# State-space scans with one state per 128 channels in place of four states by 32 channels, and a feed-forward convolution divided between TensorE quarters and VectorE

## The chip, the cores and the metric

The program runs on one core of a Trainium2 chip. The metric is the device time of one execution in microseconds (us), taken as the median over several runs. A core has a matrix engine (TensorE; PE in the profile, its weight loads PEld), a vector engine (VectorE, DVE), an activation engine (ScalarE, ACT), a general engine (GpSimd, POOL) and a queue that issues the transfers (SyncE, SP). They run side by side and wait for each other through semaphores. SBUF is the on-chip memory of 128 partitions; PSUM is the memory into which TensorE writes.

## What is computed

Four layers follow each other on an image tensor x of shape (4, 64, 128, 128), all in float32. Layers 0 and 3 hold a selective state-space model ("Mamba"): a causal short convolution, then for each of 128 inner channels a recurrence over the tokens, with 16 states per channel in layer 0 and 64 in layer 3. There are 65,536 tokens, one sequence in layer 0 and four of 16,384 in layer 3.

```python
xc = silu(conv(xh)); delta = softplus(dt @ dt_proj_w.T + dt_proj_b); A = -exp(A_log)
def step(h, t):                       # h: (128 channels, N states)
    d, b, c, u = t
    h = h * exp(d[:, None] * A) + (d * u)[:, None] * b[None, :]
    return h, h @ c
y = (ys + xc * D) * silu(z)
```

After its Mamba part layer 3 ends with a feed-forward block: 64 channels go to 256 by a matrix product, a 3x3 depthwise convolution with bias and GELU follows, and a second product goes back to 64 channels. Layer 1 (a transform with small matrix products and a gradient measure) and layer 2 (3x3 convolutions with a gate) are the same in both kernels.

## The kernel before

The tokens of a Mamba layer are cut into chunks of TC = 1024, that is 64 chunks per layer. VectorE has one instruction that runs the recurrence `h = da*h + bx` along the free dimension for 128 partitions at once (`tensor_tensor_scan`, line 346). The kernel puts four states by 32 channels on the 128 partitions. A **group** g is four states, and j counts the four blocks of 32 channels, so a chunk has 16/4*4 = 16 scans in layer 0 and 64/4*4 = 64 in layer 3. One scan and what belongs to it is called a **unit** here: 64*16 + 64*64 = 5120 units in all. A unit of before is, in `_Mamba.run`:

```python
nc.scalar.activation(da, c["dl"][j], AF.Exp, scale=self.A[:, j, g : g + 1])   # L339, ScalarE
nc.vector.tensor_mul(bx, c["du"][j], b)                                       # L341, VectorE, bx and b in PSUM
nc.vector.tensor_tensor_scan(hs, da, bx, st, ALU.mult, ALU.add)               # L346, VectorE
nc.gpsimd.tensor_copy(st, hs[:, TC - 1 : TC])                                 # L347, GpSimd
nc.gpsimd.tensor_mul(hs, hs, cb)                                              # L348, GpSimd
```

`b` and `cb` are the rows B and C of the group's four states, spread over 32 partitions each by TensorE (`_B`, line 278, into PSUM; `_C`, lines 209 and 290, copied to SBUF by ScalarE). They serve all four j of a group, and `b` has a single buffer. `_sums` (line 310) then adds the four states by a matrix product with a selection matrix, into 32 partitions of y for each j. `dl` and `du` need every channel four times, so delta and delta*xc go to a DRAM scratch and come back broadcast (512 KB transfers on the SP queue).

`prepare` makes xc, silu(z) and delta of a chunk; `behind` closes a chunk (gate, projection, normalisation, store). Both are generators: `run` advances them between the units of the chunk in hand, so that the end of chunk i-1 and the start of chunk i+1 are written between the units of chunk i. The softplus's four terms are added by TensorE (line 209 with e, u, l, pos). The order on each engine comes from a tile framework, which schedules by the order of the program's text, by dependencies and free buffers, and sets the semaphores.

`layer3_ffn` works on 32 strips of 16 image rows. For each of two halves t of 128 channels it expands (`ph`, line 1124; bias by VectorE, line 1125), applies the depthwise convolution as nine products with 128x128 diagonal matrices for each four rows (`pd`, line 1138), GELU on ScalarE (line 1145), and the way back (`po`, line 1153; bias and residual on VectorE, line 1157).

Of the kernel before, what the change touches and what calls it, by code (L numbers as in the profile page):

```python
# [17 lines left out]
P = 128  # L18
# [6 lines left out]
NQ, DD = 4, 32  # L25
ND = DI // DD
SET6 = "natural_log_exp_and_others"
# [9 lines left out]
def _const_table():  # L37
# [46 lines left out]
        "sel": np.tile(np.eye(DD), (NQ, 1)),  # L84
        "neye": -eye,
# [44 lines left out]
class _Mamba:  # L130
# [4 lines left out]

    def __init__(self, ctx, tc, K, nst, w):
        nc = self.nc = tc.nc
        self.tc = tc
        self.K, self.nst, self.ng = K, nst, nst // NQ
        cp = self.cp = ctx.enter_context(tc.tile_pool(name="mc", bufs=1))
        self.wp = ctx.enter_context(tc.tile_pool(name="mw", bufs=2))
        self.dram = ctx.enter_context(tc.tile_pool(name="md", bufs=2, space=DRAM))
        self.bp = ctx.enter_context(tc.tile_pool(name="mb", bufs=1, space=PSUM))  # L150
# [4 lines left out]
        for k in range(2):  # L155
# [12 lines left out]
        wbc = cp.tile([P, 2 * nst], F32, name="wbc")  # L168
        nc.sync.dma_start(wbc, w["xp_bcT"])
        self.spread = cp.tile([P, 2 * self.ng, NQ, DD], F32, name="spread")  # L170
        nc.vector.tensor_copy(
            self.spread.rearrange("p g q e -> p (g q) e"), wbc.unsqueeze(2).to_broadcast([P, 2 * nst, DD])
        )
# [5 lines left out]
        pm = self.pm()  # L179
# [8 lines left out]
        self.conv_b, self.dt_b = cols["conv_b"], cols["dt_b"]  # L188
        self.dD = cp.tile([P, P], F32, name="dD")
        nc.vector.tensor_scalar(self.dD, K.eye, cols["D"], None, ALU.mult)  # L190
        self.A = cp.tile([P, ND, self.ng], F32, name="A")
        with nc.allow_non_contiguous_dma(reason="the states on the partitions"):
            for q in range(NQ):
                for j in range(ND):
                    nc.sync.dma_start(
                        self.A[DD * q : DD * (q + 1), j, :],
                        w["A_log"][DD * j : DD * (j + 1), :].rearrange("e (g q) -> e g q", q=NQ)[:, :, q],
                    )
        nc.scalar.activation(self.A, self.A, AF.Exp)
        nc.vector.tensor_scalar_mul(self.A, self.A, -1.0)  # L200
        self.state = cp.tile([P, ND, self.ng], F32, name="state")

    def pm(self):
        return self.misc.tile([P, 512], F32, name="pm", tag="pm")

    def mm(self, pairs):
        pm = self.pm()
        for i, (l, r) in enumerate(pairs):
            self.nc.tensor.matmul(pm, l, r, start=i == 0, stop=i == len(pairs) - 1)  # L209
        return pm  # L210

    def t(self, name, bufs=None, w=TC):
        return self.wp.tile([P, w], F32, name=name, tag=name, bufs=bufs)


    def prepare(self, c, S, before_silu=None):

        nc, K = self.nc, self.K
        cols = [slice(512 * h, 512 * (h + 1)) for h in range(NH)]
        xc, sz = c["xc"], c["sz"] = self.t("xc"), self.t("sz")  # L220
        for h in range(NH):
            a = 512 * h
            pm = self.mm([(self.taps[0], S[:, a : a + 512]), (self.taps[1], S[:, a + 2 : a + 514])])
            nc.scalar.activation(xc[:, cols[h]], pm, AF.Identity, bias=self.conv_b)
            yield
        for h in range(NH):
            pm = self.mm([(self.wz, S[:, 512 * h + 2 : 512 * h + 514])])
            at = nc.scalar.copy(sz[:, cols[h]], pm)
            if h < NH - 1:
                yield  # L230

        tc = self.tc
        with tc.high_priority():
            if before_silu:
                at = before_silu(at)
            for t in (xc, sz):
                with tc.issue_after(at.ins):
                    at = nc.scalar.activation(t, t, AF.Silu)
            with tc.issue_after(at.ins):
                nc.scalar.preload_act_table_set(SET6)  # L240
        yield


        pos, e, l, u = (self.t(k, 1) for k in ("pos", "e", "l", "u"))
        for h in range(NH):
            pm = self.mm([(self.wdt, xc[:, cols[h]])])
            nc.scalar.activation(e[:, cols[h]], pm, AF.Abs, bias=self.dt_b)
            nc.scalar.activation(pos[:, cols[h]], pm, AF.Relu, bias=self.dt_b)
            yield
        nc.scalar.activation(e, e, AF.Exp, scale=-1.0)  # L250
        nc.scalar.activation(l, e, AF.Ln, bias=1.0)

        nc.gpsimd.tensor_scalar(u, e, 1.0, 1.0, ALU.add, ALU.subtract)
        yield
        for h in range(NH):
            k = cols[h]
            pm = self.mm([(K.eye, e[:, k]), (K.neye, u[:, k]), (K.eye, l[:, k]), (K.eye, pos[:, k])])
            nc.scalar.copy(l[:, k], pm)  # L258
            yield
        d2 = self.dram.tile([2, DI, TC], F32, name="d2", tag="d2")  # L260
        nc.sync.dma_start(d2[0], l)
        nc.gpsimd.tensor_mul(u, l, xc)
        nc.sync.dma_start(d2[1], u)
        yield
        c["dl"], c["du"] = [], []
        for j in range(ND):
            for i, (k, bufs) in enumerate((("dl", 6), ("du", 6))):
                t = self.t(k, bufs)
                nc.sync.dma_start(
                    t, d2[i, DD * j : DD * (j + 1), :].unsqueeze(0).to_broadcast([NQ, DD, TC])  # L270
                )
                c[k].append(t)
        yield


    def _spread(self, k, xc, out):
        for h in range(NH):
            self.nc.tensor.matmul(  # L278
                out(h),
                self.spread[:, k].rearrange("p q e -> p (q e)"),  # L280
                xc[:, 512 * h : 512 * (h + 1)],
                start=True,
                stop=True,
            )

    def _C(self, c, g):
        cb = self.t("cb", 2)
        for h in range(NH):
            pm = self.mm([(self.spread[:, self.ng + g].rearrange("p q e -> p (q e)"), c["xc"][:, 512 * h : 512 * (h + 1)])])
            self.nc.scalar.copy(cb[:, 512 * h : 512 * (h + 1)], pm)  # L290
        return cb

    def _B(self, c, g):
        b = self.bp.tile([P, TC], F32, name="bb", tag="bb")
        self._spread(g, c["xc"], lambda h: b[:, 512 * h : 512 * (h + 1)])
        return b

    def _sums(self, c, g, hcs):

        nc, K = self.nc, self.K  # L300
        cols = [slice(512 * h, 512 * (h + 1)) for h in range(NH)]
        if g == 0:
            c["y"] = self.bp.tile([P, TC], F32, name="y", tag="y")
        for k in cols:
            if g == 0:
                for j in range(ND):
                    e = slice(DD * j, DD * (j + 1))
                    nc.tensor.matmul(c["y"][e, k], self.dD[:, e], c["xc"][:, k], start=True, stop=False)
            for j, hc in enumerate(hcs):
                nc.tensor.matmul(  # L310
                    c["y"][DD * j : DD * (j + 1), k], K.sel, hc[:, k], start=False, stop=g == self.ng - 1
                )

    def run(self, chunks, ahead, behind):

        nc = self.nc
        for c in chunks[:1]:
            for _ in ahead(c):
                pass
        owed = None  # L320
        for i, c in enumerate(chunks):
            if c.get("reset"):
                nc.gpsimd.memset(self.state, 0.0)  # L323

            def pieces():
                if i:
                    yield from behind(chunks[i - 1])
                if i + 1 < len(chunks):
                    yield from ahead(chunks[i + 1])

            side = pieces()
            b, cb = self._B(c, 0), self._C(c, 0)
            n = 0
            for g in range(self.ng):
                hcs = []
                nxt = None
                for j in range(ND):
                    da = self.t("da", 3)
                    nc.scalar.activation(da, c["dl"][j], AF.Exp, scale=self.A[:, j, g : g + 1])  # L339
                    bx = self.bp.tile([P, TC], F32, name="bx", tag="bx")  # L340
                    nc.vector.tensor_mul(bx, c["du"][j], b)  # L341
                    if j == ND - 1 and g + 1 < self.ng:
                        b = self._B(c, g + 1)
                    hs = self.t("hs", 7)
                    st = self.state[:, j, g : g + 1]
                    nc.vector.tensor_tensor_scan(hs, da, bx, st, ALU.mult, ALU.add)  # L346
                    nc.gpsimd.tensor_copy(st, hs[:, TC - 1 : TC])  # L347
                    nc.gpsimd.tensor_mul(hs, hs, cb)  # L348
                    hcs.append(hs)
                    if j == 0 and owed:  # L350
# [910 lines left out]
```

## Time and profile before

| what | value |
|---|---|
| median of 3 runs | 30958.74 us (30957.97 to 30961.4) |
| profiled execution: its time, its span | 30961.4 us, 30959.5 us |
| busy, share of the span | PE 72%, DVE 63%, POOL 47%, ACT 32% |
| granted TensorE clock, mean | 0.823 |
| layer 0 | 0 to 5755 us |
| layers 1 and 2, first convolutions of layer 3 | 5755 to 9456 us |
| Mamba of layer 3 | 9456 to 28550 us |
| feed-forward block | 28550 to 30959.5 us |

The borders of the stages are read from the timeline, at the last or first instruction of the stage. A row of the profile that names an instruction group gives the line, the engine, the operation, output and inputs by the program's names, the shapes as partitions x elements, how often it occurred, busy time and mean duration, and the engine's idle time just before with what ended it. A float32 matrix product of the program shows as two matmul records, so counts of matmuls are twice those of the code. Durations of matmuls overlap, since they are pipelined; the distance between two starts says what one costs.

### The profile page before, as it was taken

The numbers are of one execution on the slowest core, as the hardware profiler recorded it, in microseconds if no ns is written. First come the engines' busy times: TensorE is split into PE (matmuls) and PEld (weight loads), VectorE is DVE, ScalarE is ACT, GpSimd is POOL, SyncE is SP. The second block draws the span as 40 slices with busy tenths as digits, with TensorE's granted clock in tenths as the row PEclk, the third lists the DMA queues.
The fourth block names the chain that finished last, engine by engine and source line by source line (L and its number), as shares of the span: only waits on it lengthen the run. The fifth ranks groups of instructions, "written<-read, shape, count | busy, mean of one in ns | idle before, by whom it ended". The sixth has DMA issues, their size and how long they took to land.

```text
span 30959.5 us, 165906 instructions
## 1 busy us (share of the span) xinstructions
PE 22294.9 (72%) x54602; PEld 7060.7 (23%) x54602; DVE 19538.9 (63%) x11726; ACT 10006.5 (32%) x11580; POOL 14702.2 (47%) x11431
## 2 busy tenths in 40 slices
PE   6666666378997666666666666666666666666999
PEld 1111111165442111111111111111111111111444
DVE  6666666721005777777777777777777777776111
ACT  4444444201012333333333333333333333332000
POOL 5555555600003556555555555655655556554000
PEclk8888888679998778777787777877877778777999
DMA  2111111100100000000000000000000000000000
GB/s 74 70 72 72 70 71 72 48 33 26 44 23 33 23 22 27 22 23 23 24 25 23 22 24 23 24 23 22 27 22 23 23 22 27 23 21 17 22 22 20
DMA packets 369246, 1024.19 MB, mean 33 GB/s; under 512 B 53552, under 2 KB 105984, under 8 KB 363136
## 3 DMA queue, kind: packets, MB, share of 16 engines
q1 hardware_dynamic: 368384, 1013.58, 9.6%
q8 instruction: 433, 7.09, 0.1%
q14 instruction: 429, 3.51, 0.0%
HBM read 761.78 MB, written 251.66 MB: 33 GB/s over the span
## 4 chain that ended last, share of the span: by engine, by line
PE 34%; POOL 25%; issue 12%; DVE 8%; ACT 1%; DMA 0%; SPq 0%; POOLq 0%; DVEq 0%; ACTq 0%
POOL hs L348 22%; PE y L310 7%; PE cv L859 6%; PE pd L1138 6%; PE bb L278 6%; PE pm L209 4%; DVE hs L346 3%; DVE bx L341 2%; POOL state L347 2%; PE ph L1124 1%; PE p L814 1%; PE p L803 0%; PE po L1153 0%; PE pm L379 0%; PE p L772 0%
## 5 line engine op out<-in xcount | busy, mean ns | idle before, releaser
L310 PE MATMUL y<-hs,cst 128*32 128x512 f32 x20480 | 8009.9, 708 | 6203.5 <-POOL hs L348 6199.0
L346 DVE TENSOR_TENSOR_SCAN hs<-da,state,bx 128x1024 f32<-128x1024 f32 x5120 | 12012.9, 2346 | 696.5 <-DVE bx L341 15.1
L348 POOL TENSOR_TENSOR hs<-hs,cb 128x1024 f32<-128x1024 f32 x5120 | 12029.1, 2349 | 416.0 <-POOL state L347 5.7
L341 DVE TENSOR_TENSOR bx<-du,bb 128x1024 f32<-128x1024 f32 x5120 | 6289.2, 1228 | 5628.3 <-PE bb L278 4198.6
L339 ACT ACTIVATE da<-dl,A 128x1024 f32<-128x1024 f32 x5120 | 5875.2, 1149 | 12101.0 <-DVE hs L346 10337.2
L347 POOL COPY state<-hs 128x1 f32<-128x1 f32 x5120 | 939.1, 183 | 8551.9 <-DVE hs L346 5856.6
L310 PEld LDWEIGHTS y<-hs,cst 128*32 128x32 f32 x20480 | 1108.9, 117 | 12159.7 <-POOL hs L348 10055.4
L278 PE MATMUL bb<-xc,spread 128*128 128x512 f32 x5120 | 3513.5, 821 | 109.0 <-DVE bx L341 109.0
L209 PE MATMUL pm<-xc,spread 128*128 128x512 f32 x5120 | 2598.6, 621 | 85.2 <-ACT l L258 85.2
L859 PE MATMUL cv<-img,cw 128*128 128x512 f32 x4608 | 1983.8, 593 | 54.5 <-DMA img<-d_x 47.5
L1138 PE MATMUL pd<-h,diag 128*128 128x512 f32 x4608 | 2000.0, 592 | 0.0
L290 ACT COPY cb<-pm 128x512 f32<-128x512 f32 x2560 | 1395.9, 587 | 1829.1 <-POOL hs L348 1487.0
L278 PEld LDWEIGHTS bb<-xc,spread 128*128 128x128 f32 x5120 | 1216.0, 260 | 2718.3 <-issue 2683.4
L209 PEld LDWEIGHTS pm<-xc,spread 128*128 128x128 f32 x5120 | 875.9, 190 | 1811.8 <-issue 1387.9
L859 PEld LDWEIGHTS cv<-img,cw 128*128 128x128 f32 x4608 | 872.1, 189 | 1164.2 <-issue 1156.3
L1138 PEld LDWEIGHTS pd<-h,diag 128*128 128x128 f32 x4608 | 870.9, 189 | 1076.6 <-issue 1044.1
L1113 POOL MEMSET h<- 128x18 f32 x64 | 8.3, 131 | 2239.0 <-PE pd L1138 2235.9
L323 POOL MEMSET state<- 128x64 f32 (+1 forms) x5 | 0.7, 144 | 2062.9 <-DVE tok L965 2062.8
L379 PE MATMUL pm<-yg,woT 128*64 128x512 f32 x512 | 280.5, 906 | 892.2 <-ACT cb L290 755.2
L1125 DVE TENSOR_SCALAR h<-ph,ff_fc_b 128x384 f32<-128x384 f32 (+1 forms) x384 | 232.8, 613 | 1084.6 <-PE ph L1124 957.3
L1145 ACT ACTIVATE g<-pd,ff_dw_b 128x512 f32<-128x512 f32 x256 | 175.9, 687 | 2201.7 <-PE pd L1138 2201.7
L1157 DVE SCALAR_TENSOR_TENSOR o<-po,fc2b__87239,res 128x512 f32<-128x512 f32 x64 | 48.1, 751 | 1031.1 <-PE po L1153 1031.1
(297 smaller groups left out, 12806.6 us busy)
## 6 DMA issues: line engine op xcount, KB each, us to landing
dl<-d SPq DMA_DIRECT2D x512, 512.0 KB
du<-d SPq DMA_DIRECT2D x512, 512.0 KB
d<-l SPq DMA_DIRECT2D x128, 512.0 KB
d<-u SPq DMA_DIRECT2D x128, 512.0 KB
X<-d_t SPq DMA_DIRECT2D x124, 256.0 KB
S<-in_x SPq DMA_DIRECT2D x120, 256.5 KB
res<-in_x SPq DMA_DIRECT2D x128, 128.0 KB
d_x<-o SPq DMA_DIRECT2D x128, 128.0 KB
```

Source lines behind the costliest of these rows:

```text
L209: self.nc.tensor.matmul(pm, l, r, start=i == 0, stop=i == len(pairs) - 1)
L278: self.nc.tensor.matmul(out(h), self.spread[:, k].rearrange("p q e -> p (q e)"), xc[:, 512 * h : 512 * (h + 1)], start=True, stop=True,)
L290: self.nc.scalar.copy(cb[:, 512 * h : 512 * (h + 1)], pm)
L310: nc.tensor.matmul(c["y"][DD * j : DD * (j + 1), k], K.sel, hc[:, k], start=False, stop=g == self.ng - 1)
L339: nc.scalar.activation(da, c["dl"][j], AF.Exp, scale=self.A[:, j, g : g + 1])
L341: nc.vector.tensor_mul(bx, c["du"][j], b)
L346: nc.vector.tensor_tensor_scan(hs, da, bx, st, ALU.mult, ALU.add)
L347: nc.gpsimd.tensor_copy(st, hs[:, TC - 1 : TC])
L348: nc.gpsimd.tensor_mul(hs, hs, cb)
L814: nc.tensor.matmul(p[:, l], lt[:, i, l0 + l].rearrange("p x k -> p (x k)"), Vl[:, i, l0 + l], start=i == 0, stop=i == 1,)
L859: nc.tensor.matmul(p, W[:, k, :], src[:, r + dy : r + dy + 4, dx : dx + WW], start=k == 0, stop=k == 8)
L1138: nc.tensor.matmul(pd, diag[:, t, k, :], himg[:, r + dy : r + dy + 4, dx : dx + WW], start=k == 0, stop=k == 8,)
```

## The change

The Mamba class now puts the 128 channels on the partitions and does one state at a time. A chunk again has 16 or 64 units. B and C of a state are each one row of `bc`; TensorE spreads a row over 128 partitions by a product with one column of the identity, repeated 128 times (`spread`), into a PSUM pool with three buffers of 1024 columns. The multiplication by C moves from GpSimd to VectorE and reads PSUM. The sum over states moves from TensorE to GpSimd, as an addition to y in SBUF. `bx` moves from PSUM to SBUF. The DRAM scratch and its broadcasts go. The generators go too: a chunk is written from start to end, then the next. Four instructions of softplus go from TensorE and ScalarE to GpSimd and VectorE; Silu is applied directly from PSUM, and no table is preloaded by hand.

```diff
-                    da = self.t("da", 3)
-                    nc.scalar.activation(da, c["dl"][j], AF.Exp, scale=self.A[:, j, g : g + 1])
-                    bx = self.bp.tile([P, TC], F32, name="bx", tag="bx")
-                    nc.vector.tensor_mul(bx, c["du"][j], b)
-                    if j == ND - 1 and g + 1 < self.ng:
-                        b = self._B(c, g + 1)
-                    hs = self.t("hs", 7)
-                    nc.vector.tensor_tensor_scan(hs, da, bx, st, ALU.mult, ALU.add)
-                    nc.gpsimd.tensor_copy(st, hs[:, TC - 1 : TC])
-                    nc.gpsimd.tensor_mul(hs, hs, cb)
...
+        for h in range(NH):
+            pm = mm([(self.taps[0], S[:, a : a + 512]), (self.taps[1], S[:, a + 2 : a + 514])])
+            nc.scalar.activation(xc[:, cols[h]], pm, AF.Silu, bias=self.conv_b)
...
+        for h in range(NH):
+            pm = mm([(self.wdt, xc[:, cols[h]])])
+            nc.scalar.activation(e[:, cols[h]], pm, AF.Abs, bias=self.dt_b)
+            nc.vector.tensor_scalar(pos[:, cols[h]], pm, self.dt_b, 0.0, ALU.add, ALU.max)
         nc.scalar.activation(e, e, AF.Exp, scale=-1.0)
+        nc.scalar.activation(delta, e, AF.Ln, bias=1.0)
         nc.gpsimd.tensor_scalar(u, e, 1.0, 1.0, ALU.add, ALU.subtract)
+        nc.gpsimd.tensor_sub(e, e, u)
+        nc.gpsimd.tensor_add(pos, pos, e)
+        nc.vector.tensor_add(delta, delta, pos)
+        bc = t("bc")
...
+        nc.vector.tensor_mul(du, delta, xc)
+        nc.gpsimd.tensor_scalar(y, xc, self.D, None, ALU.mult)
+        def spread(row):
+            pb = self.bcp.tile([P, TC], F32, name="pb", tag="pb")          # pool with bufs=3
+            sel = K.eye[:, row : row + 1].to_broadcast([P, P])
+            for h in range(NH):
+                nc.tensor.matmul(pb[:, cols[h]], sel, bc[:, cols[h]], start=True, stop=True)
+            return pb
+        for n in range(self.nst):
+            da = t("da", 3)
+            nc.scalar.activation(da, delta, AF.Exp, scale=self.A[:, n : n + 1])
+            bx = t("bx", 2)
+            nc.vector.tensor_mul(bx, du, spread(n))
+            hs = t("hs", 3)
+            nc.vector.tensor_tensor_scan(hs, da, bx, self.state[:, n : n + 1], ALU.mult, ALU.add)
+            hc = t("hc", 3)
+            nc.vector.tensor_mul(hc, hs, spread(self.nst + n))
+            nc.gpsimd.tensor_copy(self.state[:, n : n + 1], hs[:, TC - 1 : TC])
+            nc.gpsimd.tensor_add(y, y, hc)
+        nc.vector.tensor_mul(y, y, sz)
+        return y
+    def norm(self, x, out, width, eps, centred=None):
...
+            nc.tensor.matmul(pm[:, :width], K.cent, x, start=True, stop=True)
+            nc.vector.tensor_copy(xc[:, :width], pm[:, :width])
+        nc.gpsimd.tensor_mul(sq[:, :width], xc[:, :width], xc[:, :width])
+        nc.tensor.matmul(pv[:, :width], K.j2, sq[:, :width], start=True, stop=True)
+        _rstd(nc, sq[:, :width], pv[:, :width], eps)
+        nc.vector.tensor_mul(out, xc[:, :width], sq[:, :width])
```

`layer0` and `layer3_mamba` become plain loops: load, in layer 3 `norm` of both halves, `chunk`, projection, `norm`, store. In the feed-forward block the first 128 channels keep the diagonal products, but as 64x64 blocks on quarters of the array (row half i of the channels, column half h of the rows). The second 128 channels are convolved on VectorE by nine instructions over 16 rows each. The expansion uses halves of the rows of the array, its bias goes to ScalarE, and the next strip's expansion is written between the products of the strip in hand.

```diff
+        for k in range(9):
+            tap, wk = h1[:, dy : dy + R, dx : dx + WW], dww[:, 1, k : k + 1]
+            if k:
+                nc.vector.scalar_tensor_tensor(g1, tap, wk, g1, ALU.mult, ALU.add)
+            else:
+                nc.vector.tensor_scalar(g1, tap, wk, None, ALU.mult)
+        nc.scalar.activation(g1, g1, AF.Gelu, bias=dwb1)
...
+        for kk in range(NK):
+            pd = [dp.tile([P, 4, WW], F32, name=f"pd{i}", tag=f"pd{i}") for i in range(2)]
+            for k in range(9):
+                for h in range(2):
+                    r = 8 * kk + 4 * h + dy
+                    for i in range(2):
                         nc.tensor.matmul(
-                            pd, diag[:, t, k, :], himg[:, r + dy : r + dy + 4, dx : dx + WW],
+                            pd[i][half[h]], diag[half[i], k, :], h0[half[i], r : r + 4, dx : dx + WW],
                             start=k == 0, stop=k == 8,
                         )
+                if k % 3 == 2:
+                    next(ahead, None)
...
+            for h in range(2):
+                nc.tensor.matmul(po[half[h], h], f2, g1[:, r : r + 4, :], start=True, stop=False)
+            for i in range(2):
+                for h in range(2):
+                    nc.tensor.matmul(
+                        po[half[h], h], f2h[half[h], i, :], g0[i][half[h], kk], start=False, stop=i == 1
+                    )
```

## The prediction

> **What bounds the kernel now.** I read the page's busy shares first, then the stages as windows, then in the longest stage the waits and the timeline of VectorE. No engine is full over the span:
>
> ```profile
> PE 22294.9 (72%) x54602; PEld 7060.7 (23%) x54602; DVE 19538.9 (63%) x11726; ACT 10006.5 (32%) x11580; POOL 14702.2 (47%) x11431
> ...
> L346 DVE TENSOR_TENSOR_SCAN hs<-da,state,bx 128x1024 f32<-128x1024 f32 x5120 | 12012.9, 2346 | 696.5 <-DVE bx L341 15.1
> L348 POOL TENSOR_TENSOR hs<-hs,cb 128x1024 f32<-128x1024 f32 x5120 | 12029.1, 2349 | 416.0 <-POOL state L347 5.7
> L341 DVE TENSOR_TENSOR bx<-du,bb 128x1024 f32<-128x1024 f32 x5120 | 6289.2, 1228 | 5628.3 <-PE bb L278 4198.6
> ```
>
> The stage windows (first layer 0, then layer 3's Mamba, then the feed-forward; stretch, length, busy PE, PEld, DVE, ACT, POOL, clock, DMA) give each its own limit:
>
> ```profile
> 0.00:5755.00 5755.00, 3799.01 (x9608) 1107.45 (x9608) 3735.31 (x2125) 2398.50 (x2887) 3114.15 (x2311) 0.83 0.19 71
> ...
> 9610.00:28550.00 18940.00, 13059.53 (x28788) 3128.47 (x28788) 14667.71 (x8235) 6989.16 (x7941) 11165.88 (x8807) 0.79 0.07 23
> 28550.00:30959.50 2409.50, 2392.19 (x5888) 1048.45 (x5888) 285.71 (x474) 177.21 (x257) 14.39 (x144) 1.00 0.09 22
> ```
>
> The feed-forward is TensorE's (99%). In the Mamba layers VectorE leads at 77% and 65%. Its timeline, at the edge of a group, shows the rest:
>
> ```profile
> 20113.28 1.23 DVE L341 TENSOR_TENSOR bx<-du,bb 128x1024 f32<-128x1024 f32 x1
> 20114.64 2.35 DVE L346 TENSOR_TENSOR_SCAN hs<-da,state,bx 128x1024 f32<-128x1024 f32 x1
> 20121.64 1.23 DVE L341 TENSOR_TENSOR bx<-du,bb 128x1024 f32<-128x1024 f32 x1 [4.65 <-PE bb L278]
> ```
>
> A unit costs 3.74 us from bx to bx, and each fourth one waits for the single buffer bb. So layer 3 takes 19094/4096 = 4.66 us per unit, layer 0 5755/1024 = 5.62. The ends of chunks lie beside the units and cost VectorE almost nothing.
>
> **What the Trainium skill says.** "SBUF — State Buffer", Who interferes with whom: VectorE's second SBUF port pair is GpSimd's; a VectorE instruction with two SBUF inputs contends with a GpSimd instruction that reads SBUF, and the second to start blocks until the first has finished. The trace agrees. In layer 1's gradients both kinds meet:
>
> ```profile
> 5775.99 2.28 DVE L515 TENSOR_TENSOR gy<-d 128x2048 f32<-128x2048 f32 x1
> 5778.19 6.71 DVE L513 TENSOR_TENSOR gx<-v 128x2048 f32<-128x2048 f32 x1
> ...
> 5776.33 6.43 POOL L508 TENSOR_TENSOR v<-X 128x2112 f32<-128x2112 f32 x1
> 5782.72 6.68 POOL L511 TENSOR_TENSOR d<-X 128x2112 f32<-128x2112 f32 x1
> ```
>
> GpSimd's first (4.63 us undisturbed) runs 6.43, waiting for gy's end; then gx (2.28 alone) waits for it and takes 6.71; they take turns. In the Mamba of before bx and bb are in PSUM, each VectorE instruction has one SBUF input, and scans stay at 2345 to 2350 ns beside a busy GpSimd: no contention. "TensorE: Matmul & The Clock Gate", Part 3: products on different row and column tiles run at the same time. For column tiles the trace agrees: ten records of y<-hs on four 128x32 tiles took 1.90 us (at 200.90), where ten in a row at 0.43 cost 4.3; row tiles no run here shows. "TensorEngine Tiling (Array Packing)", Key Properties: a change of tiling mode drains the array; unpriced here.
>
> **The change, part by part.**
>
> *Unit.* VectorE gets a third instruction, hc = hs*pb, of bx's form (1228 ns). bx stays 1228 (PSUM to SBUF with yg, L369, is 1199), the scan 2346: 4.80 us. Steps between instructions add 0.03 each: 4.90. The scan now has two SBUF inputs, and GpSimd's y += hc too, so they take turns. GpSimd is free to read between two scans, 2.46 us: the addition (as L348, 2.35, of which some 2.2 hold the ports: 4.5 for 2112 elements in the gradients) and the copy of the state (0.18 to 0.26). That just fits. In the built program VectorE's steady order is bx(n+1), hc(n), scan(n+1): hc(n) releases the addition just when scan(n+1) starts. VectorE starts its next instruction 0.03 us after the last, GpSimd 0.06 after VectorE's end (20004.23 and 20004.26 after a scan's end at 20004.20), so the scan goes first, and the addition waits and fills the gap behind it. I take 4.92 us; ends 4.80 and 5.2 (the copy runs into the scan).
> Others in the unit: ScalarE 1.15, three buffers ahead. TensorE 4 products = 8 records of 0.43: 3.44 us at full clock, 4.36 at this stage's 0.79; below 4.92, with a third PSUM buffer as slack. At 0.70 it would be even. What goes (y<-hs, bb, cb, the 512 KB broadcasts) lay beside VectorE except bb's wait, 4.2 ms in all, which the third instruction's 5120 x 1.23 = 6.3 ms replaces.
>
> *Ends of chunks.* In the built program nothing of chunk i+1 stands ahead of chunk i's last unit on VectorE, ScalarE or GpSimd; only its loads are issued ahead, on SP. So the way from the last scan to the next chunk's first is uncovered; I add it up for layer 0, each step waiting for the one before: last two additions and copies on GpSimd 4.95; y*sz 1.2; projection 1.3; pc 0.75 (as L965); square on GpSimd 1.27; mean by TensorE 1.25; Ln 0.69, table load 1.28, Exp 0.63 (L123, L124); load and three Silu 3.5; sz and Abs with their products 4.4 (two pm buffers); load, Exp, load, Ln 4.8; on GpSimd u 3.64 (L253) and two additions 4.7; delta, du, bx, bx 4.9. With 0.05 per handover 37 to 40; I take 38. Layer 3 has three normalisations instead of one on this way (centre 1.1 to 1.7, copy 0.7, square 1.27, mean 1.25, Ln, load, Exp, load, partly in parallel): 52. TensorE may be at half clock here, as y's ten records took 1.90 and four of bb 3.78 at 232.55; that is in the upper ends, 44 and 60; lower ends 33 and 43.
> A chunk from first to last scan is n units less bx, bx, hc: 16*4.92-3.7 = 75.0; 64*4.92-3.7 = 311.2.
> Layer 0: 64*(75.0+38) = 7232, with 25 of setup 7257 (5755 before). Layer 3: 64*(311.2+52) = 23245, 23270 with setup (19094 before).
>
> *Feed-forward.* Before 2409/32 = 75 us per strip, of it 72 products of 0.86 = 62 for pd. After, TensorE: 72 quarters four at a time 15.5; 12 ph, two at a time, 3.9; 12 po in six steps 5.2: 25. VectorE: eight taps of 2.28 (L515's size, undisturbed, as GpSimd only fills borders), the first 1.2 to 2.3, four outputs of 0.75: 22.5 to 23.6. ScalarE: 12 biases 0.6, Gelu 1.9 and 4 x 0.69: 12. The program alternates them over strips; with waits for the single po and ph buffers I take 27: 32*27+40 = 900. Ends 760 (VectorE alone) and 1500.
>
> *The rest*, 5755 to 9456, is the same text: 3701.
>
> Sum: 7257+3701+23270+900 = 35128; rounded for the clock's play to **35,000 us**, against the profiled execution's 30961.4 (span 30959.5), which is the median 30958.74 within 0.01%. So +13%. By parts: between first and last scans 64*(75.0+311.2) = 24.7 ms, where the two layers took 24.8; ends of chunks +5.8 ms of mostly idle VectorE; feed-forward -1.5.
>
> **Rivals.**
> A, the forecast: 80%. With its ends (units -0.6/+1.4 ms, chunk ends -0.9/+0.9, feed-forward -0.1/+0.6, which don't all fall together): 34,000 to 36,500.
> B, GpSimd wins the ports: if the addition gets in before the scan each time, scan and addition stand in one row with bx and hc: 4.92+2.2 = 7.1 us. 5120*2.2 = 11.3 ms more, 46,300. For it: both are released by hc(n). Against: the 0.03 us above, and GpSimd still copies then. 7%.
> C, quarters don't overlap: pd stays at 62 us, po and ph at 18: 80 per strip, 2,560 for the block, 36,700. For: row tiles unseen here, changes of mode. Against: column tiles overlap fully. 9%.
> D, the other side: the ends of chunks are hidden after all, since the engines run apart. 128 ends are 64*(38+52) = 5.8 ms; they decide from the point where over 4.0 ms of it (70%) lie beside units; all hidden but VectorE's own 0.9 ms: 30,100. Against: each engine takes its instructions in order, and VectorE's y*sz stands ahead of the next pos. 2%.
> The last 2% are for what I don't see, spread evenly over slower outcomes and no change.
>
> **How the numbers follow.** 35,000 is A's. The range 33,900 to 36,700 takes in A and C and leaves B, D and the tails. Measurement tells 0.2% (62 us) from no change: faster 2% (D), same 1%, slower 97%.
>
> **What would show it.** Right: the windows give 7.2, 3.7, 23.2 and 0.9 ms; on L240 scans of 2.35 to 2.5 us; on L244 additions far above 2.35, up to 4.6, since they wait for the scan; per chunk one gap of VectorE's units of about 38 and 52 us; VectorE at 77% of the span. Wrong: scans of 4.5 us (B); pd records not four together (C); bx of the next chunk within 10 us of the last hc (D); VectorE waiting for pb in the unit (TensorE the bound).

## The result and the profile after

The changed kernel takes **33420.54 us** (median of 4, 33417.99 to 33422.36) against 30958.36 us (median of 4) for the kernel before on the same chip: a ratio of 1.0795, 95% interval 1.0776 to 1.0814. It is slower, as forecast, but by 8% and not by 13%: 33,420 lies below the range of 33,900 to 36,700.

The page of the changed kernel, busy shares and then its groups of the unit (busy us, mean ns, idle time just before and its releaser):

```profile
PE 25582.2 (77%) x61258; PEld 10287.3 (31%) x61258; DVE 26042.6 (78%) x18298; ACT 9045.1 (27%) x8724; POOL 24609.9 (74%) x11544
...
L244 POOL TENSOR_TENSOR y<-y,hc 128x1024 f32<-128x1024 f32 x5120 | 21393.4, 4178 | 626.2 <-DVE hc L242 121.4
...
L240 DVE TENSOR_TENSOR_SCAN hs<-da,state,bx 128x1024 f32<-128x1024 f32 x5120 | 12003.3, 2347 | 13.3
...
L242 DVE TENSOR_TENSOR hc<-hs,pb 128x1024 f32<-128x1024 f32 x5120 | 6208.6, 1215 | 17.4 <-DVE hs L240 0.5
L238 DVE TENSOR_TENSOR bx<-du,pb 128x1024 f32<-128x1024 f32 x5120 | 6129.8, 1199 | 13.3
```

The scan kept its length (2347 ns, 2346 before) and VectorE waits for next to nothing in a unit: 13 to 17 us in front of each of its three groups, over 5120 units. The addition on GpSimd takes 4178 ns, where a GpSimd product of this size took 2349 before: it is the one that waits for the shared ports, as forecast. The stage windows (stretch, length, then busy PE, PEld, DVE, ACT, POOL, clock, DMA):

```profile
0.00:6870.00 6870.00, 4856.47 (x9864) 1837.12 (x9864) 5211.69 (x3731) 2167.74 (x2116) 5197.91 (x2383) 0.89 0.04 11
6870.00:10520.00 3650.00, 2960.90 (x10140) 1750.33 (x10141) 782.03 (x856) 386.96 (x429) 344.09 (x121) 0.87 0.10 32
10520.00:32184.00 21664.00, 16800.00 (x35111) 6411.73 (x35109) 19303.56 (x13270) 6153.61 (x5634) 19052.72 (x8895) 0.95 0.02 5
32184.00:33416.00 1232.00, 964.79 (x6144) 288.14 (x6144) 745.27 (x443) 336.81 (x545) 15.16 (x145) 0.90 0.17 44
```

Forecast were 7.2, 3.7, 23.2 and 0.9 ms: the Mamba stages are shorter, the feed-forward longer. The timeline of VectorE and of GpSimd in layer 3 (start, duration) shows why the Mamba stages are shorter:

```profile
20200.50 1.22 DVE L242 TENSOR_TENSOR hc<-hs,pb 128x1024 f32<-128x1024 f32 x1
20201.63 2.35 DVE L240 TENSOR_TENSOR_SCAN hs<-da,state,bx 128x1024 f32<-128x1024 f32 x1
20203.89 1.20 DVE L238 TENSOR_TENSOR bx<-du,pb 128x1024 f32<-128x1024 f32 x1
20205.00 1.22 DVE L242 TENSOR_TENSOR hc<-hs,pb 128x1024 f32<-128x1024 f32 x1
20206.13 2.35 DVE L240 TENSOR_TENSOR_SCAN hs<-da,state,bx 128x1024 f32<-128x1024 f32 x1
...
20201.86 4.28 POOL L244 TENSOR_TENSOR y<-y,hc 128x1024 f32<-128x1024 f32 x1
20206.08 0.19 POOL L243 COPY state<-hs 128x1 f32<-128x1 f32 x1
```

From scan to scan it is 20206.13 - 20201.63 = **4.50 us**, although the three recorded durations add up to 4.77. Each instruction starts 0.09 us before the recorded end of the one ahead: the steps are 2.26, 1.11 and 1.13. The addition starts 0.23 after the scan, waits for its end and is done just when the next scan starts. GpSimd is then full (4.28 + 0.19 of 4.50), yet the scan keeps its length: whether GpSimd sets the pace all the same is tried below.

The end of a chunk in layer 0, on VectorE (the bracket is the idle time before and its releaser):

```profile
2025.59 2.35 DVE L240 TENSOR_TENSOR_SCAN hs<-da,state,bx 128x1024 f32<-128x1024 f32 x1
2028.07 1.22 DVE L242 TENSOR_TENSOR hc<-hs,pb 128x1024 f32<-128x1024 f32 x1
2032.54 1.23 DVE L245 TENSOR_TENSOR y<-y,sz 128x1024 f32<-128x1024 f32 x1 [3.24 <-POOL y L244]
...
2060.46 1.23 DVE L216 TENSOR_TENSOR delta<-delta,pos 128x1024 f32<-128x1024 f32 x1 [8.27 <-POOL pos L215]
...
2065.32 4.59 DVE L240 TENSOR_TENSOR_SCAN hs<-da,state,bx 128x1024 f32<-128x1024 f32 x2
```

From the end of the last scan (2025.59 + 2.35 = 2027.94) to the first of the next chunk it is 37.4 us, with softplus's three steps on GpSimd (3.64, 2.34 and 2.34 us) behind its longest wait. In layer 3 one such way, from 19999.66 to 20053.93, takes 54.3 us. These ways differ in length: layer 3's scans last from 10595.67 to 32166.30, and with 285.2 us from the first scan to the last in each of its 64 chunks, 52.7 us are left on the mean for each of the 63 ways between them. The forecast was 38 and 52.

### The profile page after: what moved, and what is told of

Same layout as the page of the kernel before. It is cut to its first block, busy times and chain, and to the rows that moved or that the text cites. A ratio compares the mean times of both kernels' runs of the same rounds, so it can differ in the third digit from the quotient of the medians.

```text
span 33415.9 us, 181119 instructions
## 1 busy us (share of the span) xinstructions
PE 25582.2 (77%) x61258; PEld 10287.3 (31%) x61258; DVE 26042.6 (78%) x18298; ACT 9045.1 (27%) x8724; POOL 24609.9 (74%) x11544
## 4 chain that ended last, share of the span: by engine, by line
POOL 55%; PE 10%; DVE 4%; issue 3%; ACT 2%; DMA 0%; SPq 0%; POOLq 0%; DVEq 0%; ACTq 0%
POOL y L244 52%; PE cv L718 6%; POOL state L243 2%; DVE g L992 1%; PE pm L188 1%; PE pm L269 1%; PE pm L263 1%; PE pd L1005 1%; POOL nsq L267 1%; DVE hs L240 0%; POOL e L214 0%; POOL pos L215 0%; POOL u L213 0%; PE pm L252 0%; PE ph L958 0%
## 5 line engine op out<-in xcount | busy, mean ns | idle before, releaser
L231 PE MATMUL pb<-bc,cst 128*128 128x512 f32 x40960 | 19179.3, 612 | 4751.2 <-DVE bx L238 4621.1
L244 POOL TENSOR_TENSOR y<-y,hc 128x1024 f32<-128x1024 f32 x5120 | 21393.4, 4178 | 626.2 <-DVE hc L242 121.4
L231 PEld LDWEIGHTS pb<-bc,cst 128*128 128x128 f32 x40960 | 7456.6, 192 | 16453.5 <-DVE bx L238 8542.1
L240 DVE TENSOR_TENSOR_SCAN hs<-da,state,bx 128x1024 f32<-128x1024 f32 x5120 | 12003.3, 2347 | 13.3
L236 ACT ACTIVATE da<-delta,A 128x1024 f32<-128x1024 f32 x5120 | 5852.7, 1148 | 16488.0 <-DVE hs L240 15695.2
L242 DVE TENSOR_TENSOR hc<-hs,pb 128x1024 f32<-128x1024 f32 x5120 | 6208.6, 1215 | 17.4 <-DVE hs L240 0.5
L238 DVE TENSOR_TENSOR bx<-du,pb 128x1024 f32<-128x1024 f32 x5120 | 6129.8, 1199 | 13.3
L269 PE MATMUL pm<-nsq,cst 128*128 128x512 f32 x512 | 513.2, 1104 | 500.3 <-POOL nsq L267 498.4
L213 POOL TENSOR_SCALAR u<-e 128x1024 f32<-128x1024 f32 x128 | 466.5, 3645 | 413.4 <-ACT e L209 413.4
L188 PE MATMUL pm<-S,tap 128*128 128x512 f32 x1024 | 633.9, 763 | 116.0 <-POOL S L872 110.6
L1005 PE MATMUL pd<-h,diag 64*64 64x512 f32 x4608 | 669.7, 628 | 0.7 <-issue 0.7
```

What stands on the lines that cost most here:

```text
L231: nc.tensor.matmul(pb[:, cols[h]], sel, bc[:, cols[h]], start=True, stop=True)
L236: nc.scalar.activation(da, delta, AF.Exp, scale=self.A[:, n : n + 1])
L238: nc.vector.tensor_mul(bx, du, spread(n))
L240: nc.vector.tensor_tensor_scan(hs, da, bx, self.state[:, n : n + 1], ALU.mult, ALU.add)
L242: nc.vector.tensor_mul(hc, hs, spread(self.nst + n))
L244: nc.gpsimd.tensor_add(y, y, hc)
```

## The experiments

Each was run beside the kernel before on the same chip; times are medians of 4.

### The unit: order, overlap and shared ports

**VectorE held in the order of the text**, bx, scan, hc. `issue_after` puts an instruction behind the one that it names; `prev` is the last unit's hc.

```diff
+            pb = spread(n)
+            with self.tc.issue_after(prev.ins) if prev else ExitStack():
+                nc.vector.tensor_mul(bx, du, pb)
-            nc.vector.tensor_mul(bx, du, spread(n))
...
-            nc.vector.tensor_mul(hc, hs, spread(self.nst + n))
+            prev = nc.vector.tensor_mul(hc, hs, spread(self.nst + n))
```

> The changed kernel with VectorE's three instructions of a unit held in the order bx(n), scan(n), hc(n); nothing else is changed. The scheduler's own order was bx(n+1), hc(n), scan(n+1), in which no instruction needs the result of the one just before it. Theory O (the unit came out at 4.51 us and not 4.92 because the durations of neighbours that do not depend on each other overlap): now the scan needs bx and hc needs the scan, so the unit is 1.36 (start of bx to start of its scan, as in the kernel before) + 2.35 and some 0.1 + 1.13 = 4.9 to 4.95 us. 0.4 to 0.45 us times 5120 units is 2.0 to 2.3 ms more than the changed kernel: 35,400 to 35,700 us. Rival G (GpSimd's addition and copy, 4.46 us together, set the pace, and VectorE has room): within 300 us of the changed kernel's 33,420.

Measured: 40731.49 us. Both theories missed it, by 5 ms and more. The unit takes 6.00 us, and the scan, never blocked in the changed kernel, is now the one that waits (first the group's row on the page, then the timeline):

```profile
L243 DVE TENSOR_TENSOR_SCAN hs<-da,state,bx 128x1024 f32<-128x1024 f32 x5120 | 17159.7, 3352 | 683.6 <-DVE bx L241 19.4
```

```profile
20200.06 3.38 DVE L243 TENSOR_TENSOR_SCAN hs<-da,state,bx 128x1024 f32<-128x1024 f32 x1
20203.57 1.22 DVE L245 TENSOR_TENSOR hc<-hs,pb 128x1024 f32<-128x1024 f32 x1
...
20198.94 2.35 POOL L247 TENSOR_TENSOR y<-y,hc 128x1024 f32<-128x1024 f32 x1 [1.25 <-DVE hc L245]
```

Here bx stands between hc and the scan. The addition, released by hc, is at work from 20198.94 to 20201.29; the scan starts at 20200.06, in the middle of it, and lasts 1.03 us longer. Two effects were mixed, dependent neighbours and the ports; the next run takes the ports away.

**bx in PSUM**, so that no VectorE instruction of a unit has two SBUF inputs:

```diff
-        self.bcp = ctx.enter_context(tc.tile_pool(name="mbc", bufs=3, space=PSUM))
+        self.bcp = ctx.enter_context(tc.tile_pool(name="mbc", bufs=2, space=PSUM))
-            bx = t("bx", 2)
+            bx = self.bcp.tile([P, TC], F32, name="bx", tag="bx", bufs=1)
```

> The changed kernel with bx in PSUM (one buffer), for which the pool of spread rows pb goes from three buffers to two. Every VectorE instruction of a unit then has one SBUF input at most. Theory L (the addition on GpSimd lasts 4.18 us because it waits for the scan to release the shared SBUF ports): its mean falls to 2.35 us, GpSimd's busy time by 9 ms. Theory V (VectorE paces the unit, GpSimd only just fits): the unit stays at 4.5 to 4.65 us all the same, and the total at 33,000 to 34,000 us, the ends of chunks being shorter by some 2 to 4 us each, as the last additions are. Rival G (GpSimd paces the unit): the unit falls visibly below 4.5 us and the total below 32,700. Rival P (two pb buffers are too few for TensorE): the unit grows beyond 4.7 us, as in the control with two pb buffers alone.

Measured: 35658.46 us. The addition falls to 2346 ns and GpSimd's busy time from 24610 to 15254 us, so theory L is right. The unit was missed. The scheduler chose the order hc, bx, scan here. Rival P's figure for the unit, above 4.7 us, came true, but not its cause: the rows of bx and hc show 0.5 us of waiting for pb in the whole run.

```profile
20203.63 2.35 DVE L240 TENSOR_TENSOR_SCAN hs<-da,state,bx 128x1024 f32<-128x1024 f32 x1
20206.11 1.22 DVE L242 TENSOR_TENSOR hc<-hs,pb 128x1024 f32<-128x1024 f32 x1
20207.25 1.22 DVE L238 TENSOR_TENSOR bx<-du,pb 128x1024 f32<-128x1024 f32 x1
20208.60 2.35 DVE L240 TENSOR_TENSOR_SCAN hs<-da,state,bx 128x1024 f32<-128x1024 f32 x1
```

This is the price of dependence without the ports: 2.48 from the scan to hc that reads it, 1.14 from hc to bx, 1.35 from bx to the scan that reads it, 4.97 in all. In the changed kernel's order the same three cost 4.50. So an instruction that reads what the one just before it wrote starts 0.22 us later than one that does not. With the ports the order hc, bx, scan costs another 1.03: 6.00.

**Control: two pb buffers in place of three, nothing else.**

> Control for the run with bx in PSUM: the changed kernel with two pb buffers in place of three, bx still in SBUF. If two buffers suffice, 33,420 within 150 us, additions at 4.1 to 4.3 us as before. If TensorE needs the third, VectorE waits for pb in each unit and the total rises by 5120 times the wait: 0.2 us each would be 1.0 ms.

Measured: 40732.56 us, the same as the first run, with scans of 3349 ns. What made it slow is not TensorE, it seems: with two buffers the scheduler put hc, bx, scan in a row, and the ports did the rest. That is what the next run checks.

**Two pb buffers, and the order bx(n+1), hc(n), scan(n+1) held** (bx after the last scan, hc after bx, the scan after hc).

> The control with two pb buffers once more, but with VectorE's order held at bx(n+1), hc(n), scan(n+1), as the changed kernel has it. With two buffers alone the scheduler chose hc(n), bx(n+1), scan(n+1), the unit was 6.0 us and the scan 3.35. Theory W (the order decides who gets the shared SBUF ports first: with hc directly ahead of the scan the scan is first and GpSimd's addition waits, with bx in between the addition is first and the scan waits): scans 2.35 us, additions about 4.2, units 4.5 to 4.6, 33,400 to 33,700 us. Rival P (two buffers are too few for TensorE): VectorE waits for pb in each unit, above 35,000.

Measured: 36175.35 us. Theory W is right on the ports, rival P on the total: the scans are back at 2345 ns and the additions at 4219, but bx waits for its row of pb in almost each unit (4992 times, 2246.9 us in all).

```profile
20207.85 1.22 DVE L242 TENSOR_TENSOR bx<-du,pb 128x1024 f32<-128x1024 f32 x1 [0.40 <-PE pb L231]
20208.99 1.21 DVE L247 TENSOR_TENSOR hc<-hs,pb 128x1024 f32<-128x1024 f32 x1
20210.12 2.35 DVE L252 TENSOR_TENSOR_SCAN hs<-da,state,bx 128x1024 f32<-128x1024 f32 x1
```

The unit is 5.01 us. The third buffer is worth 0.5 us, the order 1.0.

**The addition cut to one column** (y is not summed over the states).

```diff
-            nc.gpsimd.tensor_add(y, y, hc)
+            nc.gpsimd.tensor_add(y[:, :1], y[:, :1], hc[:, :1])
```

> The changed kernel with the addition over the states left out but for its first column (128x1 in place of 128x1024), so y is not summed. GpSimd then hardly touches the shared ports in a unit. Theory V (in the changed kernel's order the lock costs VectorE nothing, the unit of 4.51 us is VectorE's own): units stay at 4.51 us; only the last addition ahead of y*sz goes from each chunk, some 3 us of 128 ends, and the total is 32,850 to 33,200 us. Rival G (GpSimd's 4.28 + 0.18 us pace the unit): units fall below 4.4 us, the total below 32,700.

Measured: 33017.01 us, theory V. The unit is unchanged at 4.50, so in the changed kernel's order it is VectorE's alone. The 403 us that go match the waits of y*sz for the last addition (411.0 us in the changed kernel's table of waits). One column still waits for the scan:

```profile
L244 POOL TENSOR_TENSOR y<-y,hc 128x1 f32<-128x1 f32 x5120 | 10010.4, 1955 | 10558.8 <-DVE hc L242 10555.0
```

### The ends of chunks

**The kernel before without its interleaving**: `m.per = 0` in both layers (2 and 1 before).

> The kernel before with its interleaving taken away: the end of chunk i-1 and the start of chunk i+1 are written behind the last unit of chunk i, not between its units; nothing else is changed. The scheduler still moves some of it among the last five units. Theory E (a chunk's end and start, if not written between units, lie bare on the way): 25 to 45 us for each of 128 borders, 3.2 to 5.8 ms, 34,200 to 36,700 us. Rival R (four buffers of dl and du and the engines' slack hide them without interleaving): below 31,900.

Measured: 36593.93 us, theory E: 5,630 us more, 44 per border. In VectorE's waits (total us, times, longest), the kernel before first and then this run, it shows where: a chunk's first units need what its start makes last.

```profile
DVE bx L341 <- DMA du<-d: 1277.9, 251, 69.4
```

```profile
DVE bx L341 <- DMA du<-d: 5416.2, 512, 69.0
```

The growth of these waits for du, which comes by way of DRAM, is 4.1 of the 5.6 ms. A border of the kernel before thus holds other work than one of the changed kernel, and its 44 us are not the changed kernel's 37 and 53.

**The changed kernel's unit with the interleaving of before.** `prepare`, `behind` and `run` of before around the three VectorE instructions; u is made on VectorE.

> The changed kernel's unit (128 channels on the partitions, one state at a time, three VectorE instructions, addition on GpSimd) inside the run structure of the kernel before: the end of chunk i-1 and the start of chunk i+1 are written between the units of chunk i, the softplus is summed on TensorE, bc is copied and y started on ScalarE; the feed-forward is the changed kernel's. Theory E (the 128 ends of chunks, 37 us and 54 us, are the loss; the unit itself is no dearer than before's): the gaps close, units 5120 x 4.51 = 23.1 ms, some 2 to 4 us of VectorE's and GpSimd's side work per chunk 0.3 to 0.5 ms, layers 1 and 2 3.7 ms, feed-forward 1.23 ms: 28,300 to 29,000 us, 5 ms below the changed kernel and below the kernel before. Rival T (TensorE's granted clock falls as its idle time goes: 4 products of a unit are 3.44 us at full clock and 4.9 at 0.70): units of 4.9 to 5.5 us and VectorE waiting for pb, 30,300 to 33,400. Rival D (the side work stands in the way on GpSimd, which has 0.05 us left per unit): gaps of 10 us and more remain at the chunk's borders, 29,500 to 30,500.

Measured: 32833.42 us. None of the three is right. The clock did not fall (0.946), and bx and hc wait for pb only 241 us in all (154.7 and 85.9), so not T, although the time lies in its range. The page shows the ports again:

```profile
L293 DVE TENSOR_TENSOR_SCAN hs<-da,state,bx 128x1024 f32<-128x1024 f32 x5120 | 14386.6, 2810 | 282.2 <-DVE bx L290 8.1
```

Most scans last 2.34 or 3.38 us, in stretches, as the scheduler puts bx ahead of hc or behind it: in the trace 2842 scans directly behind hc take 2.34 on the mean, and 2212 behind bx 3.42. That is 2212 x 1.08 = 2.4 ms; the dependent neighbours of that order, at 0.47 a unit, would be another 1.0 ms. Theory E was 3.8 to 4.5 ms too low; what is left of that was not taken apart.

**The same with the order held, and GpSimd's side work moved to VectorE and ScalarE.**

> The pipelined version (ends of chunks written between the units) with VectorE's order held at bx(n+1), hc(n), scan(n+1), across the borders of chunks too, and the side work of GpSimd (normalisation products, residual additions) moved to VectorE and ScalarE. Theory W+E (order gives units of 4.51 us, interleaving hides the ends): 5120 x 4.51 = 23.1 ms, VectorE's side work 4 to 14 us per chunk 0.6 to 1.5 ms, layers 1 and 2 3.7, feed-forward 1.25: 28,700 to 29,600 us, below the kernel before by 4 to 7%. Rival S (side work shifts the addition out of its place, and the scans behind it wait again): units between 4.5 and 6 and scans of 2.8 on the mean as in the first pipelined version, 31,000 to 32,800.

Measured: 30705.94 us, ratio 0.9918 (0.9903 to 0.9933), between the two theories' figures. The order held, with scans of 2342 ns on the mean. The rest went into the side work, which was priced at 4 to 14 us per chunk. VectorE's groups between 12000 and 28000 us, in layer 3:

```profile
L978 DVE TENSOR_TENSOR S<-nxc,nsq 128x512 f32<-128x512 f32 x104 | 288.8, 2777 | 0.0
L323 DVE TENSOR_TENSOR yg<-y,sz 128x1024 f32<-128x1024 f32 x51 | 168.7, 3308 | 0.0
L993 DVE TENSOR_TENSOR xr<-xr,tr 128x512 f32<-128x512 f32 x52 | 144.6, 2781 | 0.0
L999 DVE TENSOR_TENSOR o<-nxc,o 128x512 f32<-128x512 f32 x52 | 144.1, 2771 | 0.0
L243 DVE TENSOR_SCALAR u<-e 128x1024 f32<-128x1024 f32 x51 | 141.8, 2779 | 0.0
```

A product of 128x512 that took 0.69 us at the ends of chunks in the changed kernel (L271) lasts 2.78 here: it stands behind a scan, and GpSimd's addition, which has waited for that scan, takes the ports ahead of it. So does u, with one SBUF input only: 2.78, where the run before shows 0.69 at the median. S twice, the other four and du's 1.55 are 18.7 us per chunk, waits for pb and l 4.9; 64 x 4.50 + 23.6 = 311.6, against a measured 313.6 from one yg to the next (20112.96 to 20426.56). The kernel before needs 19094/64 = 298. In layer 0 a chunk takes 88.7 us, as it does at the median in the kernel before. So in this version, with the ends hidden, a chunk is no shorter than one of the kernel before; what it gains comes from the feed-forward. Whether the side work can be placed so that it does not meet the addition was not tried.

### The feed-forward

**The kernel before with the changed `layer3_ffn` alone.**

> The kernel before with the changed kernel's feed-forward block alone. Theory F (the parts add up; a strip is 38.5 us here as there): 30,960 less 2,410 plus 1,232: 29,780 us. Rival K (the block's 38.5 us per strip come from the clock or from what the changed Mamba leaves behind, and would be the forecast 27 here): 29,450. Rival N (the feed-forward gains nothing for the whole): 30,900.

Measured: 29791.75 us (0.9623, 0.9608 to 0.9637), theory F: the parts add up. A strip of 16 rows takes 1232/32 = 38.5 us. VectorE and ScalarE of the changed kernel show what it waits for:

```profile
32598.99 7.13 DVE L992 SCALAR_TENSOR_TENSOR g<-h,dww,g 128x2048 f32<-128x2048 f32 x3
32620.16 1.29 DVE L994 TENSOR_SCALAR g<-h,dww 128x2048 f32<-128x2048 f32 x1 [14.05 <-ACT h L963]
...
32606.15 2.00 ACT L995 ACTIVATE g<-g,dwb 128x2048 f32<-128x2048 f32 x1 [8.92 <-DVE g L992]
32608.06 1.03 ACT L963 ACTIVATE h<-ph,ff_fc_b 128x384 f32<-128x384 f32 x2
```

VectorE's first tap of a strip waits 14 us for h1. ScalarE had stood 8.92 us at the wide Gelu, which needs VectorE's last tap, with h1's biases queued behind it.

**The Gelu behind the next strip's h1**, which is made ahead of h0.

```diff
-        for t in range(2):
+        for t in (1, 0):
...
-        nc.scalar.activation(g1, g1, AF.Gelu, bias=dwb1)
...
+        with tc.issue_after(H["last", 1].ins) if H else ExitStack():
+            nc.scalar.activation(g1, g1, AF.Gelu, bias=dwb1)
```

> As the run before it, but the wide Gelu of VectorE's half (g1) is held behind the biases of the next strip's second half h1, which are made ahead of those of h0. Theory A (VectorE's first tap waits 15 us in each strip because ScalarE, in its order, waits for VectorE's taps with this Gelu before it makes the next strip's h1): the wait goes, a strip is VectorE's 9 taps and 4 outputs, 24 to 28 us, 0.8 to 0.95 ms for the block, 29,320 to 29,500 us. Rival P (the single PSUM buffer of the expansion holds TensorE and with it h up): no change, 29,780 within 60.

Measured: 29831.11 us. Theory A fell: ScalarE no longer waits for g, but a strip is as long as before. The waits in the block:

```profile
DVE g L1161 <- ACT h L1130: 327.6, 32, 10.9
PEld po L1192 <- DVE o L1199: 315.2, 32, 10.4
PE po L1192 <- DVE o L1199: 287.0, 32, 9.5
```

TensorE stands 9 us per strip at po, the way back. Its single buffer is freed by VectorE's output, which is queued behind the nine taps of the next strip, and the next products and expansions are queued behind po.

**And po in two buffers of one bank** (with the late Gelu). Its output is then one VectorE instruction of 128x512 where it was two of 64x512; the second buffer and the shorter output were not tried apart.

```diff
-    op = ctx.enter_context(tc.tile_pool(name="ffo", bufs=1, space=PSUM))
+    op = ctx.enter_context(tc.tile_pool(name="ffo", bufs=2, space=PSUM))
-            po = op.tile([P, 2, 4, WW], F32, name="po", tag="po")
+            po = op.tile([P, 4, WW], F32, name="po", tag="po")
...
+            nc.vector.scalar_tensor_tensor(o[:, kk], po, b2, res[:, kk], ALU.add, ALU.add)
```

> The kernel before with the changed feed-forward, the wide Gelu held behind the next strip's h1 (as in the run that moved the wait to TensorE), and the way back po in one PSUM bank of 128 rows with two buffers, in place of two half-used banks with one buffer; its output is then one VectorE instruction of 128x512 where it was two of 64x512. Theory B (the strip waits twice in a row on single resources: first ScalarE's order, and when that is mended TensorE stands at po, whose buffer VectorE frees only after its nine taps): neither wait is left, a strip is TensorE's 25 or VectorE's 22 us, 25 to 29 us, block 0.85 to 0.95 ms, total 29,400 to 29,510 us. Rival C (a third wait takes the place, such as ph's single buffer): 29,700 or more.

Measured: **29451.59 us**, ratio 0.9512 (0.9497 to 0.9526), theory B, the fastest of all. A strip is now 27.1 us (first taps at 29109.75 and 29136.84), and the window of the block shows TensorE busy for 875 of 890 us. TensorE now sets the pace, and VectorE still waits 5.3 us per strip for h:

```profile
28559.00:29449.00 890.00, 875.02 (x6144) 267.41 (x6144) 691.27 (x377) 336.57 (x545) 13.69 (x134) 0.99 0.24 60
```

**po in two buffers without the late Gelu.**

> The run before it without the moved Gelu: po in two buffers of one bank, ScalarE's order as in the changed kernel. Theory B (ScalarE's order is a wait of its own): VectorE's first tap still waits some 13 to 15 us for h1, a strip is 36 to 38 us, 29,700 to 29,790 us. Rival D (the po buffer alone was the cause): as good as with the moved Gelu, 29,400 to 29,510.

Measured: 29767.82 us, theory B: one wait after the other, and either mend alone brings nearly nothing (24 us less, 39 us more); both together bring 340.

## Why the prediction was right and wrong

- **Sign and mechanism right.** With the ends of chunks bare the Mamba stages get longer, and the feed-forward takes back part of it.
- **The unit is the step that failed**: "4.80 us. Steps between instructions add 0.03 each: 4.90", then 4.92. It measured 4.50. The recorded durations, 4.77, were nearly right, but in an order where no instruction waits for the one just before it each starts 0.09 us before the recorded end of that one, so the steps take 0.27 off a unit and add nothing. The 0.03 was read in the kernel before:

```profile
20001.85 2.35 DVE L346 TENSOR_TENSOR_SCAN hs<-da,state,bx 128x1024 f32<-128x1024 f32 x1
20004.23 1.23 DVE L341 TENSOR_TENSOR bx<-du,bb 128x1024 f32<-128x1024 f32 x1
```

There bx has a single buffer (line 150), so each bx must wait until the scan just before it has read the last one. That this wait makes the gap is not shown apart, but fits the run with bx in PSUM: bx has one buffer there too, but hc stands in between, and bx starts 0.08 before hc's recorded end. The forecast named the right order and priced it with the gap of a chain in which each instruction waits for its neighbour. Even its low end, 4.80, leaves no room for an overlap, although its own fence shows one: gy starts at 5775.99 and lasts 2.28, to 5778.27, but gx starts at 5778.19. From the first scan to the last a chunk takes 69.0 us instead of 75.0 in layer 0 and 285.2 instead of 311.2 in layer 3: 64 x 32.0 = 2.05 ms, the whole error and more.
- **The ports right.** "The scan goes first, and the addition waits and fills the gap behind it" is what the timeline shows: the addition starts 0.23 behind the scan and lasts 4.28 in place of 2.35. "The Trainium skill" says so too (SBUF — State Buffer, Who interferes with whom): the second to start blocks until the first has finished. Rival B's blocked scans occur when bx stands between hc and the scan, at 6.00 us a unit and not at 7.1: the scan waits only for what is left of the addition, 1.03, while the dependent neighbours of that order cost another 0.47.
- **TensorE right, its clock wrong.** VectorE does not wait for pb. I had reckoned with a clock of 0.79 in layer 3; the run had 0.95. With the unit at 4.50, the forecast's 4.36 us at 0.79 would have left little room.
- **The ends of chunks right**: 37.4 and on the mean 52.7 us for 38 and 52, less than 0.01 ms off in all. A little luck is in it, since the steps listed for layer 0 add up to 39.3 before any handover, and 38 was taken. Rival D is out for this kernel. That the old structure's worth lay in hiding them is shown from the other side: without its interleaving the kernel before loses 5.6 ms.
- **The feed-forward mis-sized**: 900 forecast, 1232 measured. Quarters do work four at a time, since the 24 records of 12 quarter products take 2.81 us (rival C is out). The step that failed was "with waits for the single po and ph buffers I take 27": a strip took 38.5, and 11.4 us of it were ScalarE's order and then po's way back. With both mended it is 27.1. That this is the forecast's figure is luck: its 27 was 25 of TensorE and 2 of waits, and in the mended strip TensorE alone takes the 27.1 (from start to start pd 17.1, ph 5.1 and po 4.9, where 15.5, 3.9 and 5.2 were forecast).
- **The sum** mended by its steps: 35,128 - 2,048 (units) + 6 (ends) + 49 (what comes before the first and after the last scan of the two layers, 60.4 and 38.4 us for 25 each) + 332 (feed-forward) - 51 (layers 1 and 2) = 33,416; the span is 33415.9.

## What to carry to other kernels

Price a chain on one engine by the distance between starts in a trace with the same order and dependencies, not by the sum of durations: here 4.50, 4.97 and 6.00 us came from the same three instructions. Where two engines share ports, look at which of them starts first in the order as built, since a buffer more or less can turn it around, and hold that order by hand where it matters. When a mended wait brings nothing, look for the next one in line before giving the mend up; and before hiding work between units, price it with the ports taken.

## What was not expected of the hardware

How soon a VectorE instruction starts depends on what it needs of the one just before it. In these traces it starts 0.09 us before the recorded end of that one if it needs nothing of it, and 0.13 us after it if it reads its result: 2.26 against 2.48 us from start to start after a scan, 1.13 against 1.35 after a product. Where it overwrites the buffer that its neighbour read, as bx in the kernel before, it is 0.03 us after, at the median of 4992 such pairs. "The Trainium skill" (VectorE: DVE Perf Modes, The DRAIN you can't avoid) has the next operation wait until the pipeline is empty, or start earlier where it is not held, and found with eight copies that a semaphore after each costs nothing extra; here reading a neighbour's result costs 0.22 us, and the measurement decides. An addition of one column on GpSimd (128x1) lasts 1955 ns on the mean when it starts behind a scan: it waits for the scan's end as a full one does. TensorE's granted clock in layer 3 was 0.95 in the changed kernel and 0.79 in the kernel before, while TensorE was busy 78% (16800 of 21664) against 69% (13060 of 18940) of the stage. "TensorE: Matmul & The Clock Gate", Part 1, of the skill has the clock throttled until activity releases it, which goes in the same direction; no run here isolates it.
